# Last mixture-of-experts stage: rows asked for nine tiles ahead, and three pairs of reciprocal roots computed on VectorE

## The chip, the cores and the metric

The kernel runs on one core of one Trainium2 chip, in one launch, with all data in f32. The metric is the device time of one execution in microseconds (us), lower being better; the figure compared is the median over several executions. Five engines work beside each other and each takes its own instructions in order: TensorE (PE in the profile; PEld is its weight load), VectorE (DVE), ScalarE (ACT), GpSimd (POOL) and SyncE (SP), which here only issues transfers. GpSimd also issues transfers: the scattering and gathering ones, whose addresses come from a tile of indices.

## The reference, cut to what matters

The whole model is four layers, each an attention block and a feed-forward block, with a residual sum and a layer norm after every block. The change lies in the last feed-forward block and its norm, over 8 sequences of 256 tokens of width 256.

```python
def _layernorm(x, axis=-1, eps=1e-05):
    m = jnp.mean(x, axis=axis, keepdims=True)
    v = jnp.var(x, axis=axis, keepdims=True)
    return (x - m) / jnp.sqrt(v + eps)

def _L3_ffn_ref(hidden_states, gate, gate_up_proj, down_proj):   # 32 experts, 4 chosen per token
    ...
    routing_weights = jax.nn.softmax(router_logits.astype(jnp.float32), axis=-1)
    top_k_weights, top_k_indices = jax.lax.top_k(routing_weights, TOP_K)
    ...
    gate_up = jnp.einsum('TD,EDF->TEF', x, gate_up_proj)          # 256 -> 2 x 96
    g, u = jnp.split(gate_up, 2, axis=-1)
    gated = u * jax.nn.silu(g)
    next_states = jnp.einsum('TEF,EFD->TED', gated, down_proj)    # 96 -> 256
    next_states = (next_states * router_weights[..., None]).sum(axis=1)
    return next_states.reshape(batch_size, -1, HIDDEN)

x = _layernorm(x + _L3_ffn_ref(x, L3_ffn_gate, L3_ffn_gate_up_proj, L3_ffn_down_proj), axis=-1)
```

## The kernel before

The model runs phase after phase; the last phase is `ffn3`. Only the chosen experts of a token are computed. The 2048 tokens are taken in two groups of 1024, and each group passes through four steps.

1. `ffn3_sort` computes the router, picks four experts per token and gives each (token, expert) pair a slot in a list sorted by expert. Each expert's part of the list is filled up to whole tiles of 128 rows, so that a tile belongs to one expert, which makes 63 tiles at most; the kernel always runs 63. GpSimd then scatters the tokens' rows into a buffer in HBM, `rows`, with 32 indirect transfers (L954).
2. `ffn3_experts` runs over the 63 tiles. `fetch` (L1962) reads three tiles from `rows` in one transfer of 384 KB into `xg`, a pool of four such buffers, so twelve tiles. Then, in a pipeline written out by hand, step j does `turn(j)` (two TensorE transposes, L1973, and a VectorE copy out of PSUM to `xTg`, L1975), `up(j-1)` (two matmuls with the expert's weights, L1981, then Silu on ScalarE, L1988, and the product `h` on VectorE, L1990), `turn_back(j-2)` (a transpose, L1997, and a ScalarE copy, L1999) and `down(j-lag)` (one matmul, L2003, and a ScalarE copy to `yg`, L2011). After every third `down` a transfer writes three tiles to `outs` in HBM (L2013). `up` ends with a one-element copy called `beat` on GpSimd.
3. The weights of `down`, `w_f_down` (96x32x256, 3.1 MB), are read in eight transfers (L132) at the start of the first group's `ffn3_experts`. For this group `lag` is 8, for the second it is 4. Every `down` takes its expert's slice by a register, so the first `down` waits for all eight pieces.
4. `ffn3_combine` gathers each token's four results by indirect transfers on GpSimd (L2048, four for every tile of 128 tokens, 32 for a group), sums them with their weights and the residual on VectorE (L2054), and normalises two tiles (one sequence) at a time: `moments` takes mean and variance on VectorE (L183, L184) and then calls `rsqrt`, which is two GpSimd instructions, a `tensor_scalar` (L146) and a power of -0.5 (L147). `normed` applies the result on VectorE (L190), and SP writes the sequence out (L197).

The combine of the first group runs beside the second group's experts. The combine of the second group has nothing left beside it: it is the end of the kernel, and the gathers of tile t and the sums of tile t-1 alternate.

Order: inside `ffn3` the queues of TensorE, VectorE, ScalarE and GpSimd keep the order in which the Python text issues their work. SP is not in that list, so the order of its transfers is chosen by the scheduler of the framework, from its estimate of when each can go. Every transfer waits on a semaphore for its data and its buffer, and SP and GpSimd each use eight semaphores in rotation for their transfers, so that the ninth one waits for the first to land. When the first group's experts begin, the tail of the attention phase before (`attn3`) is still being drained: one piece of it is issued between steps, among it a chain over VectorE, GpSimd and ScalarE (L773 to L788) with three loads of ScalarE's function table, whose result `att` TensorE transposes (L795) just after the first `down`.

Of the kernel before, what the change touches and what calls it, by code (L numbers as in the profile page):

```python
# [10 lines left out]
F32 = mybir.dt.float32  # L11
BF16 = mybir.dt.bfloat16
I32 = mybir.dt.int32
U32 = mybir.dt.uint32
AF = mybir.ActivationFunctionType
ALU = mybir.AluOpType
AX = mybir.AxisListType

P = 128
# [5 lines left out]
LN_EPS = 1e-5  # L25
# [14 lines left out]
class Model:  # L40
# [132 lines left out]
        self.normed(b, r, *self.moments(r))  # L173
        self.norm_done(b)

    def moments(self, r):

        nc = self.nc
        st = self.small.tile([P, 2, 6], F32, tag="bnst", name="bnst")
        mv = self.small.tile([P, 2, 2], F32, tag="bnmv", name="bnmv")  # L180
        rstd = self.small.tile([P, 2], F32, tag="rstd", name="rstd")
        for t in range(2):
            nc.vector.bn_stats(st[:, t, :], r[:, t, :])  # L183
            nc.vector.bn_aggr(mv[:, t, :], st[:, t, :])  # L184
        self.rsqrt(rstd, mv[:, :, 1], 1.0, LN_EPS)
        return mv, rstd

    def normed(self, b, r, mv, rstd):
# [1761 lines left out]
    def ffn3_experts(self, w, g, act):  # L1950


        nc = self.nc
        rows, outs, expert, tiles = self.rows[g], self.outs[g], self.sorted[g][2], TILES[g]
        xg, xT, h, hT, er = {}, {}, {}, {}, {}

        def fetch(j):
            if j >= tiles:
                return
            n = min(3, tiles - j)  # L1960
            x = act.tile([P, 3, D], F32, tag="xg", name="xg", bufs=4)
            nc.sync.dma_start(  # L1962
                out=x[:, :n], in_=rows[j * P : (j + n) * P].rearrange("(n p) d -> p n d", p=P)
            )
            for i in range(n):
                xg[j + i] = x[:, i, :]

        def turn(j):
            if j % 3 == 0:
                fetch(j + 6)  # L1970
            pt = self.ps("t")[:, : 2 * P].rearrange("p (c q) -> p c q", c=2)
            for c in range(2):
                nc.tensor.transpose(pt[:, c, :], xg[j][:, c * P : (c + 1) * P], self.ident)  # L1973
            xT[j] = act.tile([P, 2, P], F32, tag="xTg", name="xTg", bufs=3)
            nc.vector.tensor_copy(xT[j], pt)  # L1975

        def up(j):
            er[j] = nc.tensor.value_load(expert[0:1, j : j + 1], min_val=0, max_val=31)
            ps = self.ps("a")[:, :192]
            for c in range(2):  # L1980
                nc.tensor.matmul(  # L1981
                    ps, xT[j][:, c, :], w["gup"][:, bass.ds(er[j], 1), c, :].rearrange(
                        "p o f -> p (o f)"
                    ),
                    start=(c == 0), stop=(c == 1),
                )
            sg = act.tile([P, 96], F32, tag="sg", name="sg", bufs=3)
            nc.scalar.activation(sg, ps[:, 0:96], AF.Silu)  # L1988
            h[j] = act.tile([P, 96], F32, tag="h", name="h", bufs=4)
            nc.vector.tensor_tensor(h[j], sg, ps[:, 96:192], ALU.mult)  # L1990

            beat = act.tile([1, 1], F32, tag="beat", name="beat", bufs=2)
            nc.gpsimd.tensor_copy(beat, h[j][0:1, 0:1])

        def turn_back(j):
            pt = self.ps("s")[:96, :P]
            nc.tensor.transpose(pt, h[j], self.ident)  # L1997
            hT[j] = act.tile([96, P], F32, tag="hT", name="hT", bufs=LAG)
            nc.scalar.copy(hT[j], pt)  # L1999

        def down(j):
            ps = self.ps("o")[:, :D]
            nc.tensor.matmul(  # L2003
                ps, hT[j], self.down[:, bass.ds(er[j], 1), :].rearrange("p o d -> p (o d)"),
                start=True, stop=True,
            )
            i = j % 3
            if i == 0:
                er["y"] = act.tile([P, 3, D], F32, tag="yg", name="yg", bufs=2)
            y = er["y"]  # L2010
            nc.scalar.copy(y[:, i, :], ps)  # L2011
            if i == 2 or j == tiles - 1:
                nc.sync.dma_start(  # L2013
                    out=outs[(j - i) * P : (j + 1) * P].rearrange("(n p) d -> p n d", p=P),
                    in_=y[:, : i + 1],
                )

        fetch(0)
        fetch(3)
        if self.down is None:  # L2020
            self.down = self.load(act, "f3_down", [96, 32, D], split=8)
            lag = LAG
        else:
            lag = 4
        steps = ((0, turn), (1, up), (2, turn_back), (lag, down))
        for j in range(tiles + lag):
            for i, f in steps:
                if 0 <= j - i < tiles:
                    f(j - i)
            yield  # L2030

    def ffn3_combine(self, g, act, ahead):


        nc = self.nc
        first, n = GROUPS[g]
        wt, slots, _ = self.sorted[g]
        ys, rs = {}, {}
        for t in range(2 * n + ahead):
            i = t - ahead  # L2040
            b = first + i // 2
            if t < 2 * n:
                ys[t] = act.tile([P, 4, D], F32, tag="yk", name="yk", bufs=4)
            if i >= 0 and i % 2 == 0:
                rs[b] = act.tile([P, 2, D], F32, tag="rk", name="rk", bufs=3)
            for k in range(4):
                if t < 2 * n:
                    nc.gpsimd.indirect_dma_start(  # L2048
                        out=ys[t][:, k, :], out_offset=None, in_=self.outs[g],
                        in_offset=bass.IndirectOffsetOnAxis(ap=slots[:, t, k : k + 1], axis=0),  # L2050
                    )
                if i >= 0:
                    r = rs[b]
                    nc.vector.scalar_tensor_tensor(  # L2054
                        r[:, i % 2, :], ys[i][:, k, :], wt[:, i, k : k + 1],
                        self.X[b][:, i % 2, :] if k == 0 else r[:, i % 2, :], ALU.mult, ALU.add,
                    )
                yield
            if i >= 0 and i % 2 == 1:
                m = self.moments(rs[b])  # L2060
                yield
                self.normed(b, rs[b], *m)
                self.norm_done(b)
                yield
# [228 lines left out]
```

## Time and profile before

| | |
|---|---|
| median of 3 runs | 2511.77 us (2509.81 to 2514.41) |
| the profiled execution's own time | 2512.97 us |
| its span, first to last instruction | 2511.2 us |
| mean granted TensorE clock | 0.949 |
| TensorE busy | 2192.5 us, 87% of the span |
| VectorE, ScalarE, GpSimd busy | 57%, 42%, 37% |
| first tile of the first group transposed | 2218.47 us |
| last `down` of the second group | 2450.80 us |
| gathers of the second group | 2455.27 to 2497.79 us, 32 of them |

A page of the profile gives, for one execution, the busy time of each engine, the chain of work that ended last, and groups of instructions by source line with their mean duration and what ended the idle time before them. The trace can be asked further for the waits (who waited for whom, and how long), for the chain in order of time, for a timeline of one stretch, and for the busy time and the clock granted to TensorE in any stretch. In rows of the timeline the first number is the start and the second the duration, in us. "x2" counts instructions that were merged into one row.

### The profile page before, as it was taken

How to read it: one execution, taken by the hardware profiler on the slowest of the kernel's cores; microseconds unless marked ns; L12 is line 12 of the kernel's file. 1: busy time of each engine (PE TensorE's matmuls, PEld its weight loads, DVE VectorE, ACT ScalarE, POOL GpSimd, SP SyncE). 2: the span in 40 equal slices, each digit the busy share in tenths (PEclk: the TensorE clock that was granted, in tenths of full speed). 3: DMA queues.
4: the chain of work that ended last, by engine and by line, in shares of the span. 5: the costliest groups of instructions: out<-in, count | busy, mean ns of one | idle time of the engine just before them, and what ended most of it. 6: DMA issues, size and time to landing. Idle time of an engine off the chain costs nothing. (4 is left out here: it accounts for less than half of the span.)

```text
span 2511.2 us, 36255 instructions
## 1 busy us (share of the span) xinstructions
PE 2192.5 (87%) x11960; PEld 1494.2 (60%) x12016; DVE 1431.1 (57%) x3593; ACT 1047.5 (42%) x3005; POOL 916.9 (37%) x1725
## 2 busy tenths in 40 slices
PE   7998899999999999999999999998877777678990
PEld 4554697756666666666664465555555554457780
DVE  4556486754544543544465454565888878645463
ACT  1334365453544544544432112221766755644450
POOL 1222443343433323333312321000566557833555
PEclk9999999999999999999999999999999978789995
DMA  5000411100000100000260011002000000145663
GB/s 160 1 1 1 165 44 40 59 5 4 3 3 8 47 1 1 1 1 1 74 206 1 1 51 52 1 0 103 1 2 1 1 1 26 41 125 172 213 212 96
DMA packets 92309, 120.76 MB, mean 48 GB/s; under 512 B 9757, under 2 KB 79582, under 8 KB 91102
## 3 DMA queue, kind: packets, MB, share of 16 engines
q1 hardware_dynamic: 82270, 95.75, 11.8%
q0 software_dynamic: 8192, 21.11, 2.8%
q8 instruction: 100, 1.64, 0.3%
q10 hardware_dynamic: 1664, 1.57, 0.2%
q14 instruction: 83, 0.68, 0.1%
HBM read 67.53 MB, written 50.88 MB: 47 GB/s over the span
## 5 line engine op out<-in xcount | busy, mean ns | idle before, releaser
L1391 POOL TENSOR_SCALAR p<-p,rs 128x128 f32<-128x128 f32 (+1 forms) x256 | 104.2, 425 | 294.7 <-DVE rs L1389 290.4
L1381 ACT ACTIVATE p<-ps_s,nm,rq 128x128 f32<-128x128 f32 (+1 forms) x256 | 128.0, 507 | 152.2 <-DVE nm L1379 152.2
L1309 ACT ACTIVATE sq<-ps_a 128x512 f32<-128x512 f32 x126 | 76.0, 603 | 227.2 <-PE ps_a L1301 226.9
L146 POOL TENSOR_SCALAR rsq<-bnmv 128x2 f32<-128x2 f32 x64 | 13.6, 212 | 377.5 <-DVE bnmv L184 369.9
L662 ACT ACTIVATE e<-ps_a,nm 128x128 f32<-128x128 f32 (+1 forms) x256 | 105.9, 435 | 107.7 <-DVE nm L659 98.4
L1310 DVE TENSOR_REDUCE ssk<-sq 128x4 f32<-128x512 f32 x64 | 43.8, 686 | 172.9 <-ACT sq L1309 172.9
L704 POOL TENSOR_SCALAR v<-e,r,nmd 128x128 f32<-128x128 f32 (+1 forms) x256 | 134.6, 537 | 10.0
L1301 PE MATMUL ps_a<-w_a_wq,xT 128*128 128x512 f32 x256 | 122.3, 600 | 12.4 <-DVE k L1323 9.4
L721 PE MATMUL ps_t<-ident,v 128*128 128x128 f32 x384 | 69.2, 317 | 61.7 <-DVE qT L600 29.4
L1301 PE MATMUL ps_a<-w_a_wv,xT 128*128 128x512 f32 x256 | 120.6, 593 | 1.0 <-ACT q L1334 1.0
L1981 PE MATMUL ps_a<-w_f_gup,xTg 128*128 x504 | 111.5, 345 | 11.4 <-DVE xTg L1975 6.9
L696 DVE SCALAR_TENSOR_TENSOR e<-e,c 128x128 f32<-128x128 f32 (+1 forms) x256 | 105.1, 460 | 25.5 <-POOL c L683 25.3
L1310 DVE TENSOR_REDUCE ssq<-sq 128x4 f32<-128x512 f32 x64 | 43.9, 686 | 129.8 <-ACT sq L1309 129.8
L1301 PE MATMUL ps_a<-w_a_wk,xT 128*128 128x512 f32 x248 | 116.5, 593 | 0.0
L1429 PE MATMUL ps_o<-w_a_wo,attT 128*128 128x256 f32 x512 | 111.8, 379 | 0.0
L662 ACT ACTIVATE e<-ps_s,nm 128x128 f32<-128x128 f32 (+1 forms) x256 | 106.8, 452 | 0.0
L1429 PEld LDWEIGHTS ps_o<-w_a_wo,attT 128*128 128x128 f32 x512 | 96.7, 190 | 12.8
L1163 DVE SCALAR_TENSOR_TENSOR yg<-ps_t,xg,yg 128x128 f32<-128x128 f32 x266 | 93.1, 350 | 12.7 <-PE ps_t L1152 3.9
L1368 PE MATMUL ps_s<-kT,qT 128*128 128x256 f32 (+1 forms) x512 | 100.3, 329 | 0.0
L721 PEld LDWEIGHTS ps_t<-ident,v 128*128 128x128 f32 x384 | 50.2, 163 | 81.4 <-issue 31.4
L1415 PE MATMUL ps_o<-pT,V 128*128 128x256 f32 x256 | 79.5, 392 | 19.2 <-ACT pT L120 19.2
L1981 PEld LDWEIGHTS ps_a<-w_f_gup,xTg 128*128 128x128 f32 x504 | 82.4, 197 | 22.2 <-ACT yg L2011 10.6
(410 smaller groups left out, 6041.7 us busy)
## 6 DMA issues: line engine op xcount, KB each, us to landing
rows<-zero SPq DMA_DIRECT2D x42, 384.0 KB, 4.5
xg<-rows SPq DMA_DIRECT2D x42, 384.0 KB, 5.1
outs<-yg SPq DMA_DIRECT2D x42, 384.0 KB, 3.7
w_f_gup<-in_f_gup SPq DMA_DIRECT2D x8, 768.0 KB, 8.6
w_f_w<-in_f_w SPq DMA_DIRECT2D x8, 512.0 KB, 6.3
w_f_down<-in_f_down SPq DMA_DIRECT2D x8, 384.0 KB, 8.3
w_f_up<-in_f_up SPq DMA_DIRECT2D x5, 512.0 KB, 7.3
lrows<-zero SPq DMA_DIRECT2D x12, 204.0 KB, 5.7
```

The source lines that it names most:

```text
L662: nc.scalar.activation(e[:, s, j * nk : (j + 1) * nk], sc[s][:, j, :], AF.Exp, bias=nm[:, s, j : j + 1], scale=1.0, accum_out=sums[:, s, j ...
L696: nc.vector.scalar_tensor_tensor(d[:, s, h, :], u.e[:, s, h, 1, :], u.c[:, s, h : h + 1], d[:, s, h, :], ALU.mult, ALU.add,)
L704: nc.gpsimd.tensor_scalar(u.v[:, s, h, :], d[:, s, h, :], u.r[:, s, h, 0:1], nm[:, s, h : h + 1], ALU.mult, ALU.add,)
L721: nc.tensor.transpose(ps[:, s, c, :], x, self.ident)
L1163: nc.vector.scalar_tensor_tensor(acc[j], y, c, acc[j], ALU.mult, ALU.add)
L1301: nc.tensor.matmul(ps, self.xt(u.b, t, c), w[which][:, c, u.cols], start=(c == 0), stop=(c == 1),)
L1310: nc.vector.tensor_reduce(out, sq, AX.X, ALU.add)
L1368: nc.tensor.matmul(sc[:, j, :], u.qT[:, h0 + j, qc * P : (qc + 1) * P], u.kT[:, h0 + j, 0:nk], start=(j == 0), stop=False,)
L1381: nc.scalar.activation(u.p[qc][:, h0 + j, :], sc[:, j, :], AF.Exp, bias=nm[:, j : j + 1], scale=r[:, j : j + 1], accum_out=u.sums[qc][:, h ...
L1391: nc.gpsimd.tensor_scalar(u.p[qc][:, j, :], u.p[qc][:, j, :], ri[:, j : j + 1], 1.0, ALU.mult, ALU.mult,)
L1429: nc.tensor.matmul(y[:, t, :], attTs[b][:, h, t * P : (t + 1) * P], w["wo"][:, h, :], start=(h == 0), stop=(h == 15),)
L1981: nc.tensor.matmul(ps, xT[j][:, c, :], w["gup"][:, bass.ds(er[j], 1), c, :].rearrange("p o f -> p (o f)"), start=(c == 0), stop=(c == 1),)
```

## The change

In `ffn3_experts`, `turn(j)` asks for the rows of tile j+9 where it asked for tile j+6, and three requests for rows, not two, stand in the text ahead of the eight transfers of `w_f_down`. The pool keeps its four buffers.

In `ffn3_combine`, for the second group alone and for its first three sequences, the reciprocal root of the variance is computed by the new `rsqrt_bits`: an estimate from the bits of the number (a shift and a subtraction from a constant, both on VectorE) and three Newton steps of four VectorE instructions each. With the addition of eps that is 15 VectorE instructions on 128x2 elements in the place of two on GpSimd. The last sequence, and all other norms, keep the two GpSimd instructions.

```diff
-    def moments(self, r):
+    def rsqrt_bits(self, out, v, eng):
+
+        n = v.shape[1]
+        half = self.small.tile([P, 4], F32, tag="nm", name="rsh")[:, :n].bitcast(I32)
+        self.nc.vector.tensor_scalar(half, v.bitcast(I32), 1, None, ALU.arith_shift_right)
+        self.nc.vector.tensor_scalar(
+            out.bitcast(I32), half, -1.0, float(0x5F3759DF), ALU.mult, ALU.add
+        )
+        t = self.small.tile([P, 4], F32, tag="sm", name="rst")[:, :n]
+        for _ in range(3):
+            eng.tensor_tensor(t, out, out, ALU.mult)
+            eng.tensor_tensor(t, t, v, ALU.mult)
+            eng.tensor_scalar(t, t, -0.5, 1.5, ALU.mult, ALU.add)
+            eng.tensor_tensor(out, out, t, ALU.mult)
+
+    def moments(self, r, by_bits=False):
...
-        self.rsqrt(rstd, mv[:, :, 1], 1.0, LN_EPS)
+        if by_bits:
+            v = self.small.tile([P, 4], F32, tag="rs", name="rsv")[:, :2]
+            nc.vector.tensor_scalar(v, mv[:, :, 1], LN_EPS, None, ALU.add)
+            self.rsqrt_bits(rstd, v, nc.vector)
+        else:
+            self.rsqrt(rstd, mv[:, :, 1], 1.0, LN_EPS)
...
             if j % 3 == 0:
-                fetch(j + 6)
+                fetch(j + 9)
...
-        fetch(0)
-        fetch(3)
+        for j in (0, 3, 6):
+            fetch(j)
         if self.down is None:
             self.down = self.load(act, "f3_down", [96, 32, D], split=8)
...
-                m = self.moments(rs[b])
+
+                m = self.moments(rs[b], g == 1 and i < 2 * n - 1)
```

## The prediction

> **What bounds the kernel now.** I read the page first: the engines' shares, then the chain that ended last.
>
> ```profile
> PE 2192.5 (87%) x11960; PEld 1494.2 (60%) x12016; DVE 1431.1 (57%) x3593; ACT 1047.5 (42%) x3005; POOL 916.9 (37%) x1725
> PE 7%; POOL 1%; DMA 1%; issue 1%; DVE 1%; ACT 0%; SPq 0%; POOLq 0%; DVEq 0%; ACTq 0%
> ```
>
> TensorE carries the kernel. The change touches only the last 300 us, so two places decide: where TensorE stands still in the last experts, and what runs after its last matmul. The waits of TensorE from 2080 us on give the first, and the chain in order of time shows the same place with the end.
>
> ```profile
> PE ps_t L1973 <- DMA xg<-rows: 6.9, 1, 6.9
> ```
>
> ```profile
> 2216.34 7.30 DMA w_f_down<-in_f_down
> 2223.66 12.51 DMA xg<-rows
> 2236.30 0.66 PE ps_t L1973 x2
> 2241.56 0.67 PE ps_o L2003 x2
> ...
> 2450.80 0.71 PE ps_o L2003 x2
> ...
> 2470.43 0.72 POOL rstd L147
> 2471.34 1.17 POOL yk L2048
> ```
>
> The rows of tile 6 are the third request. It was issued at 2223.66, when the first piece of the weights had landed and freed its semaphore, and landed 12.5 us later, behind 3.1 MB of weights. TensorE had finished tile 5's step at 2229.4 and waited 6.9 us. This is its only wait for rows in the stage. After 2450.80 TensorE is done and the chain runs through GpSimd's gathers. The clock granted to TensorE around the stall, in windows of time (the fields are TensorE busy, weight load, DVE, ACT, POOL, clock, DMA share, GB/s):
>
> ```profile
> 2223.50:2229.40 5.90, 4.87 (x30) 3.68 (x29) 3.11 (x11) 1.17 (x6) 1.87 (x6) 1.00 1.03 249
> 2229.40:2236.30 6.90, 0.00 (x0) 0.03 (x1) 0.91 (x3) 4.60 (x7) 2.56 (x8) 0.77 1.07 271
> 2236.30:2240.00 3.70, 3.44 (x12) 2.95 (x13) 1.10 (x3) 0.48 (x2) 0.17 (x1) 0.50 0.34 110
> ```
>
> Transfers run at 250 to 270 GB/s all through the stall, and TensorE restarts at half clock.
>
> **Part 1, the rows.** With the compiled queues of both kernels laid side by side, TensorE, ScalarE and (but for the roots) VectorE and GpSimd keep the same instructions in the same order. On SP one request moves: that for tiles 6 to 8, from behind the eight weight transfers to ahead of them. "Nine ahead throughout" changes nothing else: there are still four buffers, a request still waits for the transposes of the tile twelve before it, and the scheduler puts all later requests where they were. I cost it at nothing. The moved request needs no wait for a buffer. It passes the eight weight transfers on SP, which start one issue later (0.38 to 0.45 us) and queue behind 393 KB more, which at 260 to 350 GB/s is 1.1 to 1.5 us. In the trace the last piece was issued at 2221.9 and the longest landing took 9.3 us, so the weights were there by 2231.2, and will be by about 2232.7. Rows of tile 9 take the place of those of tile 6: as many bytes ahead of them as now ahead of the second request after the weights, all three of which had landed when transfers fell silent near 2237.8.
>
> What is late next? ScalarE and GpSimd, with the attention tail:
>
> ```profile
> 2229.71 1.28 ACT L780 ACT_TABLE_LOAD   x1
> 2232.79 1.28 ACT L1988 ACT_TABLE_LOAD   x1
> 2234.22 1.20 POOL L788 TENSOR_TENSOR att<-att,rr 128x256 f32<-128x256 f32 x2
> 2238.87 0.25 ACT L1988 ACTIVATE sg<-ps_a 128x96 f32<-128x96 f32 x1 [4.80 <-PE ps_a L1981]
> ```
>
> Their three table loads now hide in TensorE's stall. After the change TensorE does turn 6, up 5, turn back 4, turn 7 and up 6 from 2229.4 to about 2231.6 and then stands before turn back 5, which needs Silu 5: ScalarE is free at 2234.07, Silu 0.25 and the product 0.26 bring TensorE on at 2234.6, a stall of 3.0 us in place of 6.9. Then turn 8, up 7 (after the copy, 0.42) and turn back 6 put the first `down` at 2235.7 (weights there 3 us before; L788 done at 2235.4, so `att` just fits) and turn 9 at 2236.7 to 2237.0. In the trace turn 9 starts at 2242.50. At full clock that is 5.5 us gained.
>
> The clock. In the trace it changed at 2219.5, 2222.9, 2233.15 and 2240.0, steps of 3.4 us or whole multiples; a step with TensorE busy for 0.63 us led to half clock, one with 2.18 us did not. The Trainium skill (TensorE: Matmul & The Clock Gate, Part 1) has it that an idle window of about 3.4 us halves the clock and that the windows run freely. Read strictly, a 3.0 us stall never fills one, and the gain is 5.5. By the trace's 0.63 us row a window mostly idle is enough, so in perhaps two phases of three I expect about 2 us of work at half clock, costing 1 us: gain 4.3 to 5.5, and I take 4.8. From there to 2450.80 nothing is tied to absolute time: TensorE releases scatters, transfers and sorting steps, and the request at 2345.79 waits for the last scatter, which follows the tiles. I let the 4.8 us pass to the end; the range allows for losses.
>
> **Part 2, the roots.** The tail, GpSimd with VectorE's rows between:
>
> ```profile
> 2469.14 0.94 POOL L2048 DMA_INDIRECT yk<-outs,r_slots  x1 [0.30 <-issue]
> 2470.16 0.19 POOL L146 TENSOR_SCALAR rsq<-bnmv 128x2 f32<-128x2 f32 x1
> 2470.43 0.72 POOL L147 TENSOR_TENSOR rstd<-rsq,nhalf 128x2 f32<-128x2 f32 x1
> 2471.19 0.74 DVE L190 TENSOR_SCALAR X<-rk,bnmv,rstd 128x256 f32<-128x256 f32 x2 [2.64 <-POOL rstd L147]
> 2471.34 1.17 POOL L2048 DMA_INDIRECT yk<-outs,r_slots  x1 [0.19 <-issue]
> ...
> 2472.82 0.96 POOL L2048 DMA_INDIRECT yk<-outs,r_slots  x1 [0.30 <-issue]
> ```
>
> Gathers follow each other every 1.25 us and GpSimd never waits for data between them, so the tail is 32 gathers plus what is put among them. From 2469.14 to 2472.82 took 3.68 us for two gathers' 2.50: a root costs 1.18 us, 0.95 of it the root itself, the rest the slower gather behind it. Three roots go: 3 x 1.18 = 3.5 us. The fourth stays behind the last gather. GpSimd's gathers then wait for VectorE directly, for the sums of the tile four before; those are over by some 10 us.
>
> VectorE gets 15 instructions per root. Near rows: `nm` of 128x2 takes 0.16 us, `r_base` 0.17, and dependent ones in the sort follow each other every 0.20 to 0.23 us. So 15 x 0.21 = 3.2 us, where VectorE waited 2.64 us for GpSimd: the sequence is written 0.5 us later, hidden by the gathers. VectorE's work per sequence (eight gathers, 10.0 us) is 8 x 0.51 of sums, 1.2 of statistics, 3.2 and 0.74: 9.2 us. After the last such block (5.6 us from the sum before it) the sums catch up about 1.4 us before the last gather lands. Without that cover the end would move by what is over.
>
> Against the change speaks the Trainium skill (SBUF — State Buffer, "SBUF: two separate sides"): VectorE and GpSimd share a port pair, and while VectorE runs in a two-port mode GpSimd cannot write the descriptors of its gathers. By that rule six `tensor_scalar` per root (0.17 each) hold GpSimd up by 1.0 us, all 15 by 2.5: three roots would save 0.5 us, or cost 4.0. The trace: beside L190, a `tensor_scalar`, the gather took 1.17 us, and those behind other compute work with none beside them 1.07, so 0.10 per 0.74 us of it at most; beside the sums of two SBUF inputs gathers stay at 0.95. That is 0.13 per root. I take 0.4 for three, ends 0 and 7.5: 3.1 us gained.
>
> **Sum.** 4.8 + 3.1 = 7.9 us off the profiled execution's 2512.97, so 2505.1; it stood 1.2 above the median of the runs, which gives 2503.9 us.
>
> **Rivals.** A measurement of this kernel can tell about 0.2% (5.0 us) from no change.
>
> 1. Both parts work (chance 0.70): 2501.5 to 2506.5, by the clock's phase and the spread of the runs.
> 2. The rows' gain is lost, the tail's kept (0.13): another wait takes the stall's place (the weights at the first `down`, rows of tile 9), or it is given back at the change of groups, where TensorE waits 3.6 us for a `yg` buffer behind SP's request. Against it: weights are 3 us early, and the change of groups follows TensorE. 2508.7.
> 3. The tail's gain is lost, the rows' kept (0.09): the port lock in its middle. 2507.0.
> 4. Slower (0.08): VectorE becomes the bound of the tail. It has 10.0 us per sequence and 9.2 of work. From 0.27 us per added instruction it falls behind, and three roots pile up 45 x cost - 12 us, less 1.4 of slack. This eats the whole 8.3 us (4.8 + 3.5) from 0.48 us each. If each of the 18 `tensor_scalar` had to sit out a gather (1.25 us), the 45 take 28.2 us, the end is 14.8 late and 6.5 remain: 2518. Against it: L190's second half ran inside a gather without delay, and the near rows are at 0.21.
>
> **How the numbers follow.** Case 1 is the likeliest: 2503.9. The range 2501.0 to 2510.0 takes it and most of 2 and 3 and leaves out case 4. Faster by over 0.2%: case 1 and a little of 3, 0.72. Within: 2 and the rest of 3, 0.20. Slower: 0.08.
>
> **What would show it.** TensorE's wait for `xg` at tile 6 gone, a stall of about 3 us instead, put down to ScalarE or `h`; the first `down` near 2236 and the last near 2446; gathers every 1.25 us without a break, 39 us in all; VectorE's 15 rows at 0.16 us, 0.21 apart. Wrong if a new DMA wait stands at the first `down`, if gathers beside the new rows take 1.1 us or more, or if the sums run behind the gathers at the end.

## The result, and the profile after

The changed kernel takes 2506.7 us (median of 9 runs, 2505.27 to 2509.45) against 2514.18 us for the kernel before, measured beside it (9 runs, 2509.81 to 2515.04). The ratio is 0.9974, with a 95% interval of 0.9964 to 0.9984: a gain of 6.5 us, between 4.0 and 9.1. The profiled execution took 2507.06 us with a span of 2505.3 us. `ffn3` lines stand 20 higher than before: L1973 is now L1993, L2003 is L2023, L2048 is L2068.

The page's first part, engines' busy time, and its chain by engine:

```profile
PE 2196.2 (88%) x12016; PEld 1491.0 (60%) x12016; DVE 1439.7 (57%) x3638; ACT 1047.5 (42%) x3005; POOL 915.2 (37%) x1719
PE 8%; DVE 1%; DMA 1%; POOL 1%; issue 1%; ACT 1%; SPq 0%; POOLq 0%; DVEq 0%; ACTq 0%
```

VectorE has 45 instructions more and GpSimd six fewer, three roots' worth. ScalarE has come into the chain with 1%: a first sign of what is now late in the stage.

Two of TensorE's waits from 2080 us on, the longest that begin in `ffn3_experts` (waiting line and what it waited for: us in total, times, longest):

```profile
PE ps_s L2017 <- DVE h L2010: 3.6, 4, 2.8
PE ps_o L2023 <- ACT yg L2031: 3.6, 1, 3.6
```

The wait for the rows of tile 6, 6.9 us before, is not in the list. In its place stands 2.8 us for `h`, ahead of `turn_back(5)`. The wait for a `yg` buffer at the change of groups is as it was. The timeline of SyncE, ScalarE, TensorE and GpSimd shows why:

```profile
2217.48 1.52 SPq L1982 DMA_DIRECT2D xg<-rows  x3
2219.05 5.74 SPq L132 DMA_DIRECT2D w_f_down<-in_f_down  x8
...
2231.79 1.28 ACT L800 ACT_TABLE_LOAD   x1
2233.33 1.28 ACT L801 ACT_TABLE_LOAD   x1
2234.87 1.28 ACT L2008 ACT_TABLE_LOAD   x1
2236.16 0.25 ACT L2008 ACTIVATE sg<-ps_a 128x96 f32<-128x96 f32 x1
2236.31 1.20 POOL L808 TENSOR_TENSOR att<-att,rr 128x256 f32<-128x256 f32 x2
2236.76 0.32 PE L2017 MATMUL ps_s<-ident,h 128*96 128x128 f32 x1 [2.76 <-DVE h L2010]
2238.64 1.19 PE L2023 MATMUL ps_o<-w_f_down,hT 96*128 x2
2239.63 1.06 PE L815 MATMUL ps_t<-ident,att 128*128 128x128 f32 x4
2240.48 0.63 PE L1993 MATMUL ps_t<-ident,xg 128*128 128x128 f32 x2
```

Three requests leave SP ahead of the eight pieces of the weights. ScalarE's three table loads, hidden before under the wait for rows, now set the end of the stall: the Silu of tile 5 follows the third one, then come the product and TensorE. `att` is ready at 2237.5. The profile has no wait for the weights at the first `down`, but they came just in time: the last piece was issued at 2224.48 and landed 13.7 us later, at 2238.2, and the `down` began at 2238.64. The turn of tile 9 comes 19.81 us after the first transpose of the stage (2220.67); before it was 24.03 us.

Windows of the same stretch (TensorE busy, weight load, DVE, ACT, POOL, granted clock, DMA share, GB/s):

```profile
2234.96:2238.37 3.41, 1.24 (x7) 1.02 (x8) 1.17 (x4) 2.01 (x5) 2.41 (x8) 1.00 1.09 278
2238.37:2241.80 3.43, 3.43 (x14) 2.90 (x12) 0.68 (x2) 1.43 (x4) 0.17 (x1) 0.50 0.61 196
```

The clock still falls to half for one window of 3.4 us after the shorter stall. The end, in the chain in order of time and then in the timeline of one sequence of the combine:

```profile
2448.30 0.71 PE ps_o L2023 x2
2449.44 2.52 DMA outs<-yg
2452.07 0.71 issue
2452.78 1.07 POOL yk L2068
...
2491.91 2.72 DMA yk<-outs,r_slots
2494.73 0.48 DVE rk L2074
```

```profile
2465.87 0.18 DVE L199 BATCH_NORM_AGGREGATE bnmv<-bnst 128x2 f32<-128x6 f32 x1
2466.08 0.29 DVE L202 TENSOR_SCALAR rsv<-bnmv 128x2 f32<-128x2 f32 x1
2466.41 0.17 DVE L180 TENSOR_SCALAR rsh<-rsv 128x2 int32<-128x2 int32 x1
2466.69 0.94 POOL L2068 DMA_INDIRECT yk<-outs,r_slots  x1 [0.30 <-issue]
2467.20 0.42 DVE L188 TENSOR_SCALAR rst<-rst 128x2 f32<-128x2 f32 x1
2467.94 0.95 POOL L2068 DMA_INDIRECT yk<-outs,r_slots  x1 [0.30 <-issue]
2469.24 0.16 DVE L189 TENSOR_TENSOR rstd<-rstd,rst 128x2 f32<-128x2 f32 x1
2469.43 0.82 DVE L210 TENSOR_SCALAR X<-rk,bnmv,rstd 128x256 f32<-128x256 f32 x2
2470.44 1.02 POOL L2068 DMA_INDIRECT yk<-outs,r_slots  x1 [0.30 <-issue]
```

Gathers follow each other every 1.25 us through the root. From the first to the last of the 32 is 39.13 us (2452.78 to 2491.91), where it was 42.52. The root takes VectorE from 2466.08 to 2469.40, 3.3 us. One gather per root is slower, 1.01 or 1.02 us in place of 0.95: not one beside the 15 rows, but the one that starts just after `X`, when SP sends the sequence out.

The spans differ by 5.9 us. From the first transpose of the stage to the last `down`, 4.7 us went (2218.47 to 2450.80 before, 2220.67 to 2448.30 after); between first and last gather 3.4 went; and the stage began 2.2 us later, upstream of everything that the change touches. In the ten traced kernels of this study its start lies anywhere from 2217.97 to 2221.70.

### The profile page after: what moved, and what is told of

Same layout as the page of the kernel before. It is cut to its first block, busy times and chain, and to the rows that moved or that the text cites. A ratio compares the mean times of both kernels' runs of the same rounds, so it can differ in the third digit from the quotient of the medians.

```text
span 2505.3 us, 36356 instructions
## 1 busy us (share of the span) xinstructions
PE 2196.2 (88%) x12016; PEld 1491.0 (60%) x12016; DVE 1439.7 (57%) x3638; ACT 1047.5 (42%) x3005; POOL 915.2 (37%) x1719
## 3 DMA queue, kind: packets, MB, share of 16 engines
q8 instruction: 100, 1.64, 0.3%
## 6 DMA issues: line engine op xcount, KB each, us to landing
w_f_down<-in_f_down SPq DMA_DIRECT2D x8, 384.0 KB, 12.2
```

## The experiments

Unless a run says otherwise, edits are against the changed kernel. "Stage" is the time from the first transpose of the first group's experts to the turn of tile 9.

### One half each

Rows alone (all roots on GpSimd):

```diff
-                m = self.moments(rs[b], g == 1 and i < 2 * n - 1)
+                m = self.moments(rs[b])
```

> Rows moved, all roots on GpSimd as before. Theory (the two parts are independent and add): of the 8.1 us that the traces show between the first transpose of the stage and the last gather (4.7 for the rows, 3.4 for the roots), 4 to 5 us remain, ratio to before about 0.9982; from the first transpose to the start of turn 9 about 20 us instead of 24.0, and from the first to the last gather 42.5 us as before. Rival (the rows' gain comes partly from elsewhere or is eaten at the change of groups): from the first transpose to the last down of the second group still 232 us, ratio 1.000.

Measured: 0.9988 of the time before, interval 0.9981 to 0.9994 (2510.41 us against 2513.68), 3.0 us gained. No wait for rows; stage 19.58 us; gathers 42.63 us.

Roots alone:

```diff
-                fetch(j + 9)
+                fetch(j + 6)
...
-        for j in (0, 3, 6):
-            fetch(j)
+        fetch(0)
+        fetch(3)
```

> Roots on VectorE, rows as before. Theory: the gathers run unbroken, 39.1 us from the first to the last instead of 42.5, 3.4 us gained, ratio about 0.9986; the stall of 6.9 us at tile 6 is there again. Rival (VectorE's instructions hold the gathers up by the shared port): gathers above 1.0 us beside them and 40 us or more from first to last, a gain under 2.5 us.

Measured: 0.9986, interval 0.998 to 0.9993 (2509.78 us), 3.5 us gained. Gathers 39.09 us. The two ratios multiply to 0.9974, the ratio of the whole change: the halves work apart from each other, and neither is lost. But the rows bring less than the 4.8 us forecast, and the trace of this kernel, which has the old order of requests, points to the reason. TensorE's wait for rows here, and then the issue of the request for tile 6 (the first number of each row) in the profile of before and here:

```profile
PE ps_t L1993 <- DMA xg<-rows: 3.3, 1, 3.3
```

```profile
2223.66 3.65 SPq L1962 DMA_DIRECT2D xg<-rows  x3
2222.42 3.26 SPq L1982 DMA_DIRECT2D xg<-rows  x3
```

The same request in the same place cost 3.3 us here and 6.9 in the profile of before. Counted from the first transpose it left SP after 3.0 us here and after 5.2 there.

### Nine ahead without the moved request

Against the kernel before:

```diff
-                fetch(j + 6)
+                fetch(j + 9)
...
         else:
             lag = 4
+        fetch(6)
```

> Only the words nine ahead: every turn asks for tile j+9, but the third request stands behind the weights of down, and all roots are on GpSimd. Its compiled queues are those of before, instruction by instruction. Theory (only the moved request counts; the length of the stall at tile 6 depends on where the free-running clock windows fall at the start of the stage, which differs between executions of the same code): ratio 1.000, a wait of TensorE for rows of 3 to 7 us at tile 6, and 22 to 24 us from the first transpose to turn 9. Rival (asking nine ahead helps later tiles): ratio below 0.999 and less than 231 us from the first transpose to the last down.

Measured: 1.0001, interval 0.9993 to 1.001 (2513.66 us against 2513.1). Its queues, waits included, are those of the kernel before, so this is also a second profile of the old order. Its wait for the rows of tile 6, and the two stretches at half clock (fields as above):

```profile
PE ps_t L1973 <- DMA xg<-rows: 4.5, 1, 4.5
```

```profile
2220.75:2227.60 6.85, 5.91 (x22) 4.80 (x21) 2.44 (x8) 2.05 (x4) 0.69 (x3) 0.50 1.05 260
2234.35:2241.25 6.90, 4.84 (x17) 4.27 (x18) 1.36 (x4) 2.90 (x7) 2.35 (x7) 0.51 0.58 183
```

Why does the same stall last 6.9, 3.3 and 4.5 us (before, roots alone, here)? Counted from the first transpose, TensorE was done with tile 5 after 10.9, 11.6 and 11.4 us, the request for tile 6 left SP after 5.2, 3.0 and 3.4 us, and TensorE had its rows after 17.8, 14.9 and 15.9 us. Most of the difference is in the rows: the request goes out as soon as the first piece of the weights has landed and freed its semaphore, and that piece took 7.3, 5.6 and 5.8 us. Why it took longer in the profile of before stays open. TensorE's own part is 0.5 to 0.7 us: here and in roots alone it began the stage with two windows at half clock (2220.75 to 2227.60, and 2219.80 to 2226.62), in the profile of before with one. So of this run's two theories the first holds (the words "nine ahead" alone bring nothing), and the other, that the phase of the clock sets the length of the stall, covers only this smaller part.

Over the three traces with the old order the stage takes 24.03, 21.96 and 22.56 us (mean 22.85). Over six with the moved request it takes 19.81, 19.58, 19.99, 20.13, 20.21 and 21.02 (mean 20.12; the power experiment below, which changes the stage's own work, is left out). The gain at tile 9 is 2.7 us in the mean. The 21.02 is that of three `yg` buffers, whose edit touches nothing before the first `down`: it alone of the six began with two windows at half clock (2219.45 to 2226.27), and its stall ended 16.8 us after the first transpose instead of 16.1 or 16.2. An estimate from these few profiles: where the stage begins with one such window the moved request brings 4.1 us (24.03 against a mean of 19.94), where it begins with two, 1.2 us (22.26 against 21.02). From the first transpose to the beginning of the last row of `down`s the means are 230.1 us with the old order and 227.5 with the moved request (three `yg` buffers left out, since its edit acts before that point): 2.6 us gained, and the timed 3.0 of rows alone beside it.

### How much VectorE can carry in the tail

Nine Newton steps in each root, 24 more VectorE instructions per root:

```diff
-        for _ in range(3):
+        for _ in range(9):
```

> The changed kernel with nine Newton steps in place of three in the three roots on VectorE, 39 instructions each. Theory (VectorE has 10.0 us per sequence and now about 6.0 + 39 x 0.2 = 13.8 us of work, so it is the bound and three sequences pile up): the end comes 3 x 3.8 - 1.4 = 10 us later than in the changed kernel, ratio to before about 1.001; the gathers themselves stay 1.25 us apart until they meet buffers not yet summed. Rival (the added instructions lie beside the gathers whatever their number, GpSimd alone sets the tail): no more than 2 us later.

Measured: 1.0019, interval 1.0011 to 1.0027 (2518.06 us): slower than before. The timeline of its last us:

```profile
2490.56 1.13 POOL L2068 DMA_INDIRECT yk<-outs,r_slots  x1 [0.30 <-issue]
2491.99 1.13 POOL L2068 DMA_INDIRECT yk<-outs,r_slots  x1 [0.30 <-issue]
2505.33 1.53 DVE L2074 SCALAR_TENSOR_TENSOR rk<-yk,r_w,rk 128x256 f32<-128x256 f32 x3
2507.76 0.18 DVE L199 BATCH_NORM_AGGREGATE bnmv<-bnst 128x2 f32<-128x6 f32 x1
2508.04 0.19 POOL L146 TENSOR_SCALAR rsq<-bnmv 128x2 f32<-128x2 f32 x1 [14.91 <-DVE bnmv L199]
```

The gathers still take 39.12 us from first to last, and no gather beside a root took over 0.95 us, so the instructions beside them do not hold GpSimd up. The two shown, at 1.13 us, lie beside sums that have piled up; why they are longer is not shown. The sums do not follow: the last statistics come 15.77 us after the last gather begins, in the changed kernel 4.20. The end is 11.6 us later. By the prediction's formula for rival 4, 117 instructions at the 0.20 us they follow each other here are 23.4, less 12 and 1.4, 10.0 us. The mechanism of the rival is real; with three Newton steps VectorE still keeps up.

All four roots on VectorE:

```diff
-                m = self.moments(rs[b], g == 1 and i < 2 * n - 1)
+                m = self.moments(rs[b], g == 1)
```

> The changed kernel with the root of the last sequence on VectorE as well. Nothing lies beside the last root. Theory (an uncovered root costs its own length): from the end of the last statistics to the normalising of the last sequence 3.3 us (15 instructions, 0.2 apart, and the wait) instead of 1.2, so about 2 us slower than the changed kernel, ratio to before about 0.9982. Rival (the hop to GpSimd and back, and its instructions, cost as much as the 15): no difference from the changed kernel.

Measured: 0.9964, interval 0.995 to 0.9977 (5 runs, 2505.67 us). It overlaps the changed kernel's, and the forecast of 0.9982 lies outside it: the timed runs do not show the loss. The timeline of its end, and below it two rows of the changed kernel's end:

```profile
2499.78 0.18 DVE L199 BATCH_NORM_AGGREGATE bnmv<-bnst 128x2 f32<-128x6 f32 x1
2500.00 0.17 DVE L202 TENSOR_SCALAR rsv<-bnmv 128x2 f32<-128x2 f32 x1
2502.98 0.73 DVE L210 TENSOR_SCALAR X<-rk,bnmv,rstd 128x256 f32<-128x256 f32 x2
```

```profile
2496.11 0.18 DVE L199 BATCH_NORM_AGGREGATE bnmv<-bnst 128x2 f32<-128x6 f32 x1
2497.42 0.73 DVE L210 TENSOR_SCALAR X<-rk,bnmv,rstd 128x256 f32<-128x256 f32 x2 [1.13 <-POOL rstd L147]
```

From the last statistics to `X` takes 3.20 us here and 1.31 with GpSimd's root in the changed kernel. With nothing beside it the root by bits is 1.9 us dearer in these two profiles. Five runs do not settle a difference of that size: their median stands 1.0 us below the changed kernel's, and both intervals are over 2 us wide to either side.

### What is late next in the stage

Four requests ahead of the weights, in a single execution:

```diff
-            if j % 3 == 0:
+            if j % 3 == 0 and j:
...
-        for j in (0, 3, 6):
+        for j in (0, 3, 6, 9):
```

> The changed kernel with four requests for rows, not three, ahead of the weights. Theory (ScalarE ends the stall, and the weights have about 2 us to spare at the first down): the weights land 1.2 to 1.5 us later and TensorE waits for them 0 to 0.5 us, turn 9 within 0.7 us of 19.8 us after the first transpose. Rival (the moved request was paid for by the weights): a wait for the weights of over 1 us at the first down.

Measured: 2506.83 us; stage 20.21 us against 19.81. The timeline at the first `down`:

```profile
2237.91 1.19 PE L2023 MATMUL ps_o<-w_f_down,hT 96*128 x2 [0.17 <-DMA xg<-rows]
```

The releaser is named after rows, but what this matmul reads and TensorE had not waited for yet is `w_f_down`, whose last piece was issued at 2225.6, 12.3 us before. But nine Newton steps, with three requests, had a wait of 0.26 us in the same place (the `down` at 2237.45, the last piece issued at 2224.92), so the 0.17 us cannot be put down to the fourth request. The room ahead of the first `down` is used up in some executions already with three; so far it costs nothing that shows.

The table loads taken away: in the last sequence of `attn3` the root of the mean square is a power on GpSimd, without Ln and Exp on ScalarE.

```diff
+            if b == NB - 1:
+                for qc in range(2):
+                    g.tensor_tensor(rr[:, qc, :], ms[:, qc, :], self.nhalf, ALU.pow)
+            else:
+                nc.scalar.activation(rr, ms, AF.Ln)
+                nc.scalar.activation(rr, rr, AF.Exp, scale=-0.5)
...
```

> The changed kernel, and in the last sequence of the attention phase the logarithm and exponential on ScalarE with one Newton step (and with them three loads of the function table) are replaced by two powers of -0.5 on GpSimd. Theory (after the change the stall before turn back 5 is ScalarE's three table loads): that wait of 2.8 us is gone, TensorE runs on to the first down and stands there 0 to 2 us for the weights, which land about 16 us after the first transpose; turn 9 starts 16.5 to 18 us after the first transpose instead of 19.8, the whole 2 to 3 us faster than the changed kernel, ratio to before about 0.9962. Rival (the result att, not ScalarE, is what TensorE ends up waiting for, since GpSimd's chain is as long): turn 9 still 19 us or more after the first transpose, no gain.

Measured: 0.9983, interval 0.9976 to 0.9991 (2508.27 us): no better than the change, where 2 to 3 us more were forecast. The timeline of GpSimd and TensorE:

```profile
2231.95 5.77 POOL L802 TENSOR_TENSOR rr<-ms,nhalf 128x16 f32<-128x16 f32 x2
2237.16 0.96 PE L2027 MATMUL ps_o<-w_f_down,hT 96*128 x2 [3.07 <-DMA xg<-rows]
2237.69 1.20 POOL L812 TENSOR_TENSOR att<-att,rr 128x256 f32<-128x256 f32 x2
2238.36 1.27 PE L819 MATMUL ps_t<-ident,att 128*128 128x128 f32 x4 [0.24 <-POOL att L812]
2239.43 0.63 PE L1997 MATMUL ps_t<-ident,xg 128*128 128x128 f32 x2
```

The stall behind the table loads is gone, and TensorE waits 3.07 us at the first `down` instead. Again `xg<-rows` is named and `w_f_down` is what the matmul reads, 12.5 us after its last piece was issued (2224.67; it landed 12.0 us later, at 2236.7). `att`, delayed by the two powers, then comes 0.24 us late in its turn. Tile 9's turn is at 19.98 us after the first transpose, as with the change, and the clock then stays at half for two windows (2237.40 to 2244.23) where the changed kernel had one. So weights and `att` stand close behind the table loads, and taking away the loads alone brings nothing. A root cheaper than the two powers was not tried; the weights alone would still have held TensorE.

A third `yg` buffer for the change of groups:

```diff
-                er["y"] = act.tile([P, 3, D], F32, tag="yg", name="yg", bufs=2)
+                er["y"] = act.tile([P, 3, D], F32, tag="yg", name="yg", bufs=3)
```

> The changed kernel with three buffers for the results on their way to HBM instead of two. Theory (at the change of groups TensorE waits 3.6 us for such a buffer, since its transfer stands on SP behind a request for rows that waits for the last scatter): the wait of 3.6 us at down is gone, what is late next is the rows of the second group, which land about 2 us earlier than TensorE now takes them; 1.5 to 3 us faster than the changed kernel, ratio to before about 0.9964. Rival (the rows of the second group are as late as the buffer): a wait of over 3 us for rows in its place, no gain.

Measured: 0.998, interval 0.9972 to 0.9989 (2507.48 us), not apart from the change, where 1.5 to 3 us more were forecast. Its timeline at the change of groups:

```profile
2340.43 4.12 PE L2023 MATMUL ps_o<-w_f_down,hT 96*128 x14
2346.02 1.12 PE L1993 MATMUL ps_t<-ident,xg 128*128 128x128 f32 x4 [1.46 <-DMA xg<-rows]
2347.52 1.64 PE L2001 MATMUL ps_a<-w_f_gup,xTg 128*128 x4 [0.38 <-DVE xTg L1995]
```

The 3.6 us for `yg` are gone. The rows of the second group stand behind them with 1.5 us, so the first turn of that group comes 1.9 us sooner, counted from the start of the last row of `down`s (5.59 us for 7.48). But the first four tiles then run at half clock (`up` in 1.64, 1.49, 1.62 and 1.49 us), in the changed kernel only the first two (1.65 and 1.41, then 0.82), and the group's first `down` comes at 15.15 us from that row where it came at 14.1. The timed runs show that the gain does not arrive. That the clock takes it is read from one profile; how long it stays at half there differs without this edit too (in all four roots the third tile's `up` still takes 1.17 us).

## Why the prediction was right, and where it was not

It forecast 7.9 us off, and faster. The ratio says 6.5 us, the medians 7.5. By its number alone the result, 2506.7 us, lies just past the end of case 1 (2506.5) and nearer to rival 3 (2507.0) than to the forecast; that both parts work is known from the halves and their traces, not from the time. The absolute figure of 2503.9 us was 2.8 too low, and most of that is the base: it was worked from a median of 2511.77 us over three runs, and over nine the kernel before stands at 2514.18.

**The rows: right mechanism, wrong size.** Stall gone, 2.8 us (forecast 3.0) behind the third table load and Silu 5 in its place, ended 16.1 us after the stage began, which is the forecast 2234.6 to within 0.1 us when counted from the stage's start. The first `down` came 18.0 us after that start (forecast 17.2) and turn 9 at 19.8 (18.2 to 18.5 at full clock), through the half-clock window. Between these two profiles the term was 4.7 us, as forecast at 4.8; that it fits so well is luck, since it is 2.6 to 3.0 us in the mean. The step that failed is "gain 4.3 to 5.5, and I take 4.8": it took the 6.9 us stall of one profiled execution for that of the median run. The same order of requests had 3.3 and 4.5 us in two other profiles, most of it because the request for tile 6 left SP 1.8 to 2.2 us earlier in the stage. The sum was also moved from the profile to the median by a single 1.2 us, though this stall is just where executions differ. That the roots brought a little more than forecast (3.4 to 3.5 for 3.1) made up for part of it.

**The clock.** The Trainium skill (TensorE: Matmul & The Clock Gate, Part 1) was read strictly as letting a 3.0 us stall pass without loss, as it fills no window. The measurement decides against that reading: the window from 2234.96 to 2238.37 had TensorE busy for 1.24 us and was followed by half clock, and so was its like in each of the other five kernels with the moved request and the table loads (0.53 to 1.37 us). The row of 0.63 us that the prediction set against the rule was the better guide; "two phases of three" was too low, it was six of six.

**The weights.** The prediction has them "there 3 us before", from a longest landing of 9.3 us. That figure covers two of the eight pieces: in the trace of before only the first and the third have a recorded landing (7.3 and 9.3 us), the last has none. In the two other profiles with the old order the last piece landed 12.2 and 13.3 us after its issue, and in the changed kernel 13.7, at 2238.2. The first `down` at 2238.64 came 0.46 us after that; where TensorE did wait for the weights (nine Newton steps, the power experiment), it began 0.4 to 0.5 us after the last landing too, so in the profiled execution there was next to no room. In rows alone, three `yg` buffers and all four roots the last landing lay 2.0 to 3.3 us ahead of the first `down`. It did no harm that shows. Rival 2 (the gain lost to the weights or given back at the change of groups) falls: rows alone kept 3.0 us. It lives on in the power experiment, where the weights' wait did take the stall's place.

**Nine ahead throughout, at nothing.** Right: 1.0001, 0.9993 to 1.001.

**The roots.** Forecast 3.1 (3.5 less 0.4 for the port); the gathers became 3.4 us shorter and roots alone gained 3.5. Rows at 0.16 to 0.17 us, 0.20 apart, 3.3 us per root: as forecast. The port lock (the Trainium skill, SBUF — State Buffer, "SBUF: two separate sides") cost at most 0.07 us per root, the one gather at 1.02 behind `X`, where 0.13 was put in and the strict reading 1.0 to 2.5 us. Rival 3 falls. No gather beside a root became longer.

**VectorE as the bound.** The idle time before the last two sums is 0.46 and 0.50 us, so 1.0 us of cover where 1.4 was forecast; it was enough. Nine steps went over the edge by 11.6 us.

## What to carry to other kernels

A stall that ends with a transfer is the difference of two times, when the data lands and when the engine arrives, and both vary between executions: one profile gives one draw of it, so take several before sizing its removal. Before calling a transfer early, see whether its own landing is recorded, or only that of its neighbours. When a stall is taken away, list all that was hidden under it with its own ready time; here table loads, weights and an attention tail stood close behind each other, and removing one of them alone gained nothing. In a tail bound by one engine's issue, small work belongs on the neighbour as long as that neighbour keeps slack per round, and back on the first engine behind its last round: 15 instructions cost nothing that shows under the gathers, and in the profiles 1.9 us more than GpSimd's two behind them.

## What the hardware showed unexpectedly

- TensorE's clock fell to half after windows of 3.4 us in which it had worked for 0 to 1.37 us, and not after windows with 2.19 (before, 2222.91 to 2226.32) or 2.21 (changed, 2231.55 to 2234.96). It could stay at half for two windows: in nine-ahead-only the first one, 2220.77 to 2224.18, had TensorE busy for 2.79 us and half clock went on to 2227.6, while in the changed kernel a first window with the same 2.79 us (2221.30 to 2224.71) was followed by full clock. What tells the two apart stays open.
- In each root of the changed kernel one 128x2 `tensor_scalar` of VectorE took 0.42 us, where the same row took 0.17 in later steps, and the addition of eps 0.25 to 0.29. These six rows all begin 0.51 to 0.69 us into a gather and end within 0.02 us of its end (2467.62 us against 2467.63 for the row shown above), while rows that begin 0.3 us into one take 0.17. It looks as if the two engines do collide, but with VectorE waiting for the last part of GpSimd's gather, the other way round from what the prediction feared. One row of all four roots, 0.52 us into a gather (2490.84), took 0.17 all the same, and no run moved the rows against the gathers, so this is not shown as the cause.
- GpSimd's power took 0.72 us on 128x2 and 2.9 us on 128x16 (5.77 for two).
